# A gated graph network followed by graph attention: the product of softmax weights and rows of h in three passes

## The chip, the core and the metric

The kernel runs on one core of a Trainium2 chip. The metric is the device time of one execution in microseconds (us). One execution was also recorded by the hardware profiler; the profile and the trace below are of that execution.

A core has several engines that run side by side, each through its own instructions in a fixed order: PE (TensorE, the matrix unit), PEld (its weight loads, which overlap its products), ACT (ScalarE), DVE (VectorE), POOL (GpSimd), and SP (SyncE), which here issues DMA transfers. An engine waits at an instruction until the data it needs have been announced by the others; whatever stands behind that instruction on the same engine waits too. PSUM, the memory that PE writes, has eight banks here, each 128 x 512 floats.

## The reference

There are 64 graphs of 256 nodes with 256 features each, in float32. A first layer is a gated graph network of three steps, a second one is attention over the graph's edges; each has a normalization in front and adds its result to x. Cut to what matters:

```python
h = relu(layernorm(x))
for i in range(3):
    m    = h @ weight[i]
    aggr = einsum('bst,bsd->btd', A, m)          # A: adjacency, 0 or 1
    h    = gru_cell(aggr, h, w_ih, w_hh, b_ih, b_hh)
x = x + h

h  = relu(layernorm(x))
hW = einsum('bnd,od->bno', h, W)
e  = leaky_relu((hW @ a_left)[:, :, None] + (hW @ a_right)[:, None, :])
e  = where(adj == 0, -1e9, e)
alpha = softmax(e, axis=-1)
x = x + einsum('bij,bjd->bid', alpha, hW)
```

The kernel uses that alpha @ (h @ W.T) is (alpha @ h) @ W.T. The product of the softmax weights with the rows of h is called *mix* in the code, the following product with W *project*.

## The kernel before

The 64 graphs go through in 32 pairs (G = 2 graphs to a pair, N = 256 nodes, D = 256 features). A tile of 128 partitions by 512 elements holds one graph (two blocks of 128 nodes by 256 features) or half of the features of a pair.

Per pair, `pair(p)` records about these operations, none of which runs when it is recorded:

- `norm_relu` of the input and, for three layers, the state h split into parts (`split16`, names "h0", "h1"), the adjacency product ("prop", line 802, two per layer), its result split ("g0", "g1"), and the gates of the recurrent cell (`gate`, whose products are all line 665): per block of features r, nh, ni and z, with the arithmetic on ACT (lines 687, 820, 830, 833) and on DVE (lines 825, 828, 837 to 841).
- the attention part: `norm_relu` ("mid"), the dot products with the attention vectors (line 896), leaky relu, mask, maximum and exponentials of the scores, then a DMA transposition of the exponentials ("p turn") followed by two gathers and a copy on ACT that puts the two 16-bit halves of each number together ("p copy", the `join` of line 710). Its result is the tile `pT`: the turned, not yet normalized softmax weights.
- "mix" (line 953): for each of the two graphs, four float32 products of 128 x 128 weights (blocks of h, the tile `hb`) with 256 columns (of `pT`), summed in one PSUM bank, `pg`. The trace has two records for each float32 product of this kind.
- "c": `pg` split by `split16`: a part rounded to float32r on ACT (line 616), a float16 remainder on DVE (line 622), and a scaled float16 copy of the whole on ACT (line 627).
- "project" (line 964): the product with W in three passes, 4 products of float32r and 8 of float16, each of 256 columns. DVE multiplies the result with the reciprocal row sums, adds x (line 980), and the rows go out.

A *split in three passes* replaces a float32 product a*b by a0*b0 in float32r (a number rounded to fewer bits, in a 32-bit tile) plus two float16 passes for the remainders: a1 (the remainder of a) times a float16 copy of b, and the other way round. All gates, prop (with one float16 pass, since A is 0 or 1) and project work in this way before the change; mix doesn't. In a group with passes of both kinds (`mixed=True`), the order of the kinds alternates from group to group, so that PE switches type once in each group; the Python flag `narrow` keeps the state.

The last two pairs (p of 30 and 31, "late" and "last") use plain float32 for mix and for project (line 975), and the last pair has a code of its own (lines 1006 and 1014).

What sets the order: all operations go into a `Plan`, which is a list scheduler that runs when the kernel is built. It knows an assumed cost for each operation (the constants `MM`, `PROP`, `A512` and so on, in ns), the operations that each one needs, and the buffers ("full" 28, "round" 22, "half" 40, "bank" 8). It repeatedly takes the operation that can start first and, among equals, the one with the earliest due time; the table `LEAD` shifts the due time of operations by name. The result is a fixed sequence for each engine, and pairs overlap each other in it. So a changed cost or lead doesn't cost anything by itself: it moves instructions.

The core of the lines that the change replaces:

```python
            def mix(g=g, pT=pT, pg=pg):                                   # line 950
                for db in range(DB):
                    for jb in range(NB):
                        nc.tensor.matmul(...)                             # line 953
            pe(f"mix {g}", 4 * MM, mix, r=[(pT, ALL), (hb[g], ALL)], w=[(pg, ONE)])
            if p < NPAIR - 2:
                cs = split16(f"c{g}", pg, UP_V, True)
```

Of the kernel before, what the change touches and what calls it, by code (L numbers as in the profile page):

```python
# [10 lines left out]
F32 = mybir.dt.float32  # L11
# [19 lines left out]
    "A": -111500, "A16": -23000, "G": -500, "b_nh": -3500, "b_rz": 1000, "b_rz half": 7500, "back 0": 27500,  # L31
    "back 0 gather": 88000, "back 0 of 0": 32000, "back 0 of 1": 18000, "back 1": 28500, "back 1 gather": -33000,
    "back 1 of 0": -500, "back 1 of 1": 20500, "back copy 0": -80500, "back copy 1": -5000, "c0 0": -2500,
    "c0 1": 36500, "c0 d": 32000, "c1 1": 4000, "c1 d": 7000, "d add 0": -4000, "d add 0 of 0": -16000,
    "d add 1 of 0": -44000, "d add 1 of 1": -16000, "d mul 0": 125000, "d mul 0 of 0": -18500, "d mul 0 of 1": -5500,
    "d mul 1": 89000, "d mul 1 of 0": -24000, "d mul 1 of 1": -36000, "d sub 0": -17500, "d sub 0 of 0": -3000,
    "d sub 0 of 1": -19500, "d sub 1": -9000, "d sub 1 of 0": -38000, "d sub 1 of 1": 5500, "dot 0": -136000,
    "dot 1": 3500, "exps 0": 20000, "exps 0 0": 93000, "exps 1": 1000, "exps 1 0": -65000, "exps 1 1": -11500,
    "fill": 4000, "first A": 9000, "first A16": -17000, "first back 0": -34000, "first back 1": 16000,
    "first c0 0": -23000, "first c0 1": -26500, "first c0 d": 84500, "first c1 0": -83500, "first c1 1": -28500,  # L40
    "first c1 d": -2000, "first d add 0": 7000, "first d add 1": -4000, "first d mul 0": -84500,
    "first d mul 1": -6000, "first d sub 0": -44000, "first d sub 1": 1000, "first dot 1": 17500,
    "first exps 0": 8000, "first exps 1": -4000, "first fill": 35000, "first g0 0": -7000, "first g0 1": 69000,
    "first g0 d": -1000, "first g1 0": -8000, "first g1 1": 89500, "first g1 d": -21000, "first h0 0": 46000,
    "first h0 1": -4000, "first h0 d": 38000, "first h1 0": 44000, "first h1 1": -44500, "first h1 d": 32000,
    "first hi 0": -5500, "first hi 1": 10000, "first in 0 eps": -165000, "first in 0 pow": -11500,
    "first in 0 relu": 500, "first in 0 shift": 38000, "first in 0 stats": -16500, "first in 1 eps": -17000,
    "first in 1 pow": 2000, "first in 1 relu": 17000, "first in 1 shift": -21000, "first in 1 stats": 16000,
    "first in hi 0": -78500, "first in hi 1": 8000, "first in lo 1": 44500, "first leaky 0": 48000,
    "first leaky 1": -1500, "first line 0": -10000, "first line 1": 54000, "first lo 1": 76000, "first load": -18000,  # L50
    "first mask 0": 113000, "first mask 1": 32500, "first max 0": 16500, "first max 1": 9000,
    "first mid 0 eps": -31500, "first mid 0 pow": 3500, "first mid 0 relu": -5000, "first mid 0 shift": 500,
    "first mid 0 stats": 20500, "first mid 1 eps": -15000, "first mid 1 relu": 13000, "first mid 1 shift": -15000,
    "first mid 1 stats": 6000, "first mix 1": -29000, "first nh 0 scale": 32000, "first nh 1 scale": 8500,
    "first ni 0 topF": 28500, "first out 1": 4000, "first p copy 0": -72000, "first p copy 1": -25000,
    "first p turn 0 gather": -21000, "first p turn 1": -66000, "first p turn 1 gather": -1500,
    "first project 0": 32000, "first project 1": -3000, "first prop 0": 21000, "first prop 1": -12000,
    "first r 0 topF": -55500, "first r 0 topT": -47000, "first r 1": 31500, "first r 1 topF": 16000,
    "first r 1 topT": -52000, "first recip": 14500, "first res 0": 3500, "first right 0": 26000, "first store": -3500,
    "first tanh 0": -51500, "first tanh 1": -8000, "first total": -32000, "first turn 0": -153500,  # L60
    "first turn 1": 34500, "first turn copy 0": 33500, "first u 0": 12000, "first u 1": 16000, "first u add 0": -500,
    "first u add 1": -21500, "first z 0": -24000, "first z 0 topF": -32000, "first z 1": -33000,
    "first z 1 topF": -33500, "g0 0": 108000, "g0 1": 251500, "g0 d": 500, "g1 0": 6000, "g1 d": -49000,
    "h0 0": 39500, "h0 1": 50500, "h1 0": -43000, "h1 1": 311000, "h1 d": 112000, "hi 0": 3000, "hi 1": -7000,
    "in 0 eps": 39000, "in 0 pow": -1000, "in 0 relu": -124000, "in 0 stats": -49000, "in 1 eps": 7500,
    "in 1 pow": 17000, "in 1 relu": 19000, "in 1 shift": -14500, "in 1 stats": 323500, "in hi 0": -36000,
    "in hi 1": 40000, "in lo 0": -4000, "in lo 1": 33500, "last A": 18500, "last A16": 500, "last back 0": -94000,
    "last back 0 of 0": 1000, "last back 0 of 1": -1000, "last back 1": 24000, "last back 1 of 0": -55500,
    "last d add 0": 71500, "last d add 0 of 1": 27000, "last d add 1": 13000, "last d add 1 of 0": -2000,
    "last d add 1 of 1": 25000, "last d mul 0 of 0": 19000, "last d mul 0 of 1": -8000, "last d mul 1": -149500,  # L70
    "last d mul 1 of 0": -500, "last d mul 1 of 1": 6000, "last d sub 0": -34500, "last d sub 0 of 0": 7000,
    "last d sub 0 of 1": 37000, "last d sub 1": -20000, "last d sub 1 of 0": -74500, "last d sub 1 of 1": -111000,
    "last dot 0": -74000, "last dot 1": -7500, "last exps 0 0": 3000, "last exps 0 1": 1000, "last exps 1 0": -33500,
    "last exps 1 1": 120000, "last g0 0": -2500, "last g0 1": -30000, "last g0 d": -16000, "last g1 0": -50000,
    "last g1 1": 9000, "last g1 d": -39500, "last h0 0": -23500, "last h0 1": -33500, "last h0 d": -22000,
    "last h1 0": 41500, "last h1 1": 95500, "last h1 d": 31000, "last hi 0": 25500, "last hi 1": 16000,
    "last in 0 eps": -12000, "last in 0 pow": 34000, "last in 0 shift": 98000, "last in 0 stats": -52000,
    "last in 1 eps": -8000, "last in 1 pow": 87500, "last in 1 relu": 500, "last in 1 shift": -77500,
    "last in hi 0": -16500, "last in hi 1": 65000, "last in lo 0": -8000, "last in lo 1": 16000,
# [254 lines left out]
def tile_gated_gnn_then_gat(  # L334
# [106 lines left out]

    MM, TR, PROP, PASS = 432, 109, 120, 233
    PROP16, PASS16 = 110, 216
    A512, V512, S512, VP256, C512 = 475, 605, 660, 392, 522
    LINE, SPREAD, T16 = 4800, 4800, 1300
    SPLIT = 4096.0
    C = 1.0 / SPLIT
# [611 lines left out]
```

## Time and profile before

| What | Value |
|---|---|
| median of 3 runs (lowest to highest) | 1970.34 us (1968.96 to 1971.46) |
| the profiled execution's own time | 1970.78 us |
| its span, from first to last instruction | 1969.0 us |
| instructions in the span | 30480 |
| mean granted clock of TensorE | 0.997 |
| busy: DVE, ACT, POOL | 1548.4 us (79%), 1543.8 us (78%), 193.7 us (10%) |
| DMA, mean | 122 GB/s |

How to read it: the page gives each engine's busy time as a share of the span, then groups of like instructions (line of the code, engine, operation, tile written and tiles read, shape, count, total and mean time, idle time before them and what ended it), the waits, and the *chain*: the work that ended last, followed back from the last instruction to what released each step. Matmuls are pipelined, and a record's own duration covers its passage through the array; what a product takes of PE is the distance to the start of the next, and a piece of the chain gives that for a whole group. The trace can also be cut into windows of time with the busy time of each engine in each, and be listed in order of time.

### The profile page before, as it was taken

The page shows a single profiled execution, that of the slowest core. Times are in us where ns is not written, and L with a number is a line of the kernel's source. Part 1 is how long each engine was busy: PE and PEld are TensorE (multiplying, and loading weights), DVE is VectorE, ACT ScalarE, POOL GpSimd, SP SyncE. Part 2 cuts the span into 40 slices and gives each one's busy share as a digit, 9 for nine tenths or more (in the row PEclk, how much of TensorE's full clock was granted, in tenths as well). Part 3 has the DMA queues.
Part 4 walks back from the last instruction along what each step waited for, and adds up shares of the span by engine and source line. Part 5 has one row for each costly group of instructions (what it writes and reads, how often), then busy time and mean ns, then how long its engine had stood idle before and what let it go on. Part 6 is the DMA issues. An engine that isn't in the chain of part 4 may idle for free.

```text
span 1969.0 us, 30480 instructions
## 1 busy us (share of the span) xinstructions
PE 1953.8 (99%) x9965; PEld 1210.8 (61%) x9965; DVE 1548.4 (79%) x3714; ACT 1543.8 (78%) x2653; POOL 193.7 (10%) x262
## 2 busy tenths in 40 slices
PE   8999999999999999999999999999999999999998
PEld 5556665666665666656666656666656666566667
DVE  7687778778788777788787787787887787887776
ACT  5577887778887778887778887788777788777865
POOL 1001011011010011010010110110100110100000
PEclk9999999999999999999999999999999999999999
DMA  4256776667776687876687776677666768656632
GB/s 122 45 101 125 134 136 115 118 122 142 145 127 110 116 138 133 140 129 112 119 137 142 134 125 109 125 139 147 125 108 120 139 132 142 129 108 125 114 75 60
DMA packets 734463, 239.36 MB, mean 122 GB/s; under 512 B 658256, under 2 KB 734304, under 8 KB 734304
## 3 DMA queue, kind: packets, MB, share of 16 engines
q1 hardware_dynamic: 734272, 237.41, 65.8%
q8 instruction: 78, 1.28, 0.3%
q14 instruction: 81, 0.66, 0.2%
q10 hardware_dynamic: 32, 0.01, 0.0%
HBM read 61.09 MB, written 16.84 MB: 40 GB/s over the span
## 4 chain that ended last, share of the span: by engine, by line
PE 97%; DVE 2%; ACT 1%; issue 0%; DMA 0%; ACTq 0%; DVEq 0%
PE bank L665 77%; PE bank L802 9%; PE bank L953 6%; PE bank L964 4%; PE bank L592 0%; PE bank L868 0%; PE bank L519 0%; PE bank L975 0%; PE bank L1006 0%; PE bank L1014 0%; DVE full L839 0%; DVE full L544 0%; ACT full L738 0%; DMA rows<-in_L_gnn_b_hh_dram 0%; DVE full L841 0%
## 5 line engine op out<-in xcount | busy, mean ns | idle before, releaser
L665 PE MATMUL bank<-half,low_hh 128*128 128x512 f16 (+1 forms) x2328 | 613.9, 379 | 0.0
L665 PE MATMUL bank<-half,low 128*128 128x512 f16 (+1 forms) x2328 | 606.0, 378 | 0.0
L665 PE MATMUL bank<-round,fac_hh 128*128 128x512 f32 (+1 forms) x1164 | 398.7, 432 | 0.0
L665 PE MATMUL bank<-round,fac 128*128 128x512 f32 (+1 forms) x1164 | 393.5, 428 | 0.0
L710 ACT COPY full<-full 128x1024 uint16<-128x1024 uint16 x304 | 349.6, 1159 | 44.7 <-DMA full<-full 38.8
L665 PEld LDWEIGHTS <-low 128*128 128x128 f16 x2328 | 214.3, 98 | 273.9 <-issue 44.4
L665 PEld LDWEIGHTS <-low_hh 128*128 128x128 f16 x2328 | 198.4, 98 | 283.3 <-issue 101.5
L665 PEld LDWEIGHTS bank<-round,fac 128*128 128x128 f32 x1164 | 214.6, 189 | 58.1
L665 PEld LDWEIGHTS bank<-round,fac_hh 128*128 128x128 f32 x1164 | 214.5, 189 | 57.0
L732 POOL TENSOR_TENSOR small<-small,nhalf 128x2 f32<-128x2 f32 x128 | 103.8, 811 | 1456.8 <-DVE small L730 1398.3
L820 ACT ACTIVATE full<-bank,b_rz 128x512 f32<-128x512 f32 (+1 forms) x194 | 131.7, 680 | 104.7 <-PE bank L665 102.3
L833 ACT ACTIVATE full<-bank,b_rz 128x512 f32<-128x512 f32 (+1 forms) x194 | 131.8, 679 | 93.8 <-PE bank L665 93.4
L620 DVE TENSOR_TENSOR half<-bank,round 128x512 f16<-128x512 f32 x192 | 132.0, 688 | 75.2 <-ACT round L616 26.6
L825 DVE SCALAR_TENSOR_TENSOR full<-full,bank 128x512 f32<-128x512 f32 (+1 forms) x194 | 131.5, 678 | 61.2 <-ACT full L820 58.9
L830 ACT ACTIVATE full<-full,vec 128x512 f32<-128x512 f32 (+1 forms) x194 | 135.1, 710 | 56.1 <-DVE full L828 56.1
L616 ACT ACTIVATE round<-bank 128x512 fp32r<-128x512 f32 x252 | 150.9, 599 | 32.6 <-PE bank L802 31.5
L839 DVE SCALAR_TENSOR_TENSOR full<-full,full 128x512 f32<-128x512 f32 (+1 forms) x194 | 132.1, 681 | 55.1 <-ACT full L833 52.4
L652 DVE SCALAR_TENSOR_TENSOR half<-full,round 128x512 f16<-128x512 f32 x184 | 125.7, 684 | 57.5 <-ACT round L651 57.5
L627 ACT ACTIVATE half<-bank 128x512 f16<-128x512 f32 x252 | 144.5, 598 | 8.7 <-DVE half L620 6.3
L687 ACT ACTIVATE bank<-bank,b_nh 128x512 f32<-128x512 f32 (+1 forms) x194 | 125.6, 648 | 25.8 <-PE bank L665 25.5
L837 DVE TENSOR_TENSOR full<-full,full 128x512 f32<-128x512 f32 (+1 forms) x194 | 141.3, 739 | 4.3 <-ACT full L830 4.2
L828 DVE TENSOR_TENSOR full<-full,bank 128x512 f32<-128x512 f32 (+1 forms) x194 | 128.4, 673 | 17.5 <-PE bank L665 14.8
(106 smaller groups left out, 2465.9 us busy)
## 6 DMA issues: line engine op xcount, KB each, us to landing
full<-full SPq DMA_DIRECT2D x484, 128.0 KB, 3.5
x<-in_x_dram SPq DMA_DIRECT2D x64, 256.0 KB, 3.4
adj<-in_adj_dram SPq DMA_DIRECT2D x64, 256.0 KB, 3.4
full<-in_x_dram SPq DMA_DIRECT2D x64, 256.0 KB, 4.2
full<-full SPq DMA_DIRECT2D x248, 64.0 KB, 2.7
out_dram<-full SPq DMA_DIRECT2D x62, 256.0 KB, 2.9
full<-line SPq DMA_DIRECT2D x62, 128.0 KB, 4.3
full<-full SPq DMA_TRANSPOSE x304, 3.6
```

What stands on the lines that cost most here:

```text
L616: act(name + " 0", A512 if bank else C512, lambda: nc.scalar.activation(v0.t, v.t, AF.Copy, scale=up), r=[(v, ALL)], w=[(v0, ONE)])
L620: rem = lambda: nc.vector.tensor_sub(v1.t, v.t, v0.t.bitcast(F32))
L627: act(name + " d", A512, lambda: nc.scalar.activation(vd.t, v.t, AF.Copy, scale=up * C), r=[(v, ALL)], w=[(vd, ONE)])
L665: return [(j, lambda start, j=j, kb=kb: nc.tensor.matmul(bank.t[:, cols], fs(j, kb), s[kb][j].t[:, cols], start=start, stop=True, skip_gro ...
L710: act(name, 1065, lambda: nc.scalar.copy(dst.t.bitcast(U16).rearrange("p (j n b) -> p j n b", j=2, b=2), src.t.bitcast(U16).rearrange(f"p ...
L802: nc.tensor.matmul(pa.t[:, ts(g, N)], b, m[:, ts(sb, N)], start=(n == 0), stop=True, skip_group_check=True)
L820: act(f"r {db}{of}", fit(575, part), lambda b=r_, k=pr, db=db, cols=cols: nc.scalar.activation(b.t[:, cols], k.t[:, cols], AF.Tanh, bias=b ...
L825: dve(f"u {db}{of}", fit(S512, part), lambda u=u, k=ph, b=r_, cols=cols: nc.vector.scalar_tensor_tensor(u.t[:, cols], b.t[:, cols], 1.0, k ...
L830: act(f"tanh {db}{of}", fit(615, part), lambda u=u, en=en, cols=cols: nc.scalar.activation(u.t[:, cols], u.t[:, cols], AF.Tanh, bias=b_i[: ...
L833: act(f"z {db}{of}", fit(575, part), lambda b=z_, k=pz, db=db, cols=cols: nc.scalar.activation(b.t[:, cols], k.t[:, cols], AF.Tanh, bias=b ...
L837: dve2(f"d sub {db}{of}", fit(V512, part), lambda u=u, d=d, cols=cols: nc.vector.tensor_sub(d.t[:, cols], d.t[:, cols], u.t[:, cols]), r=[ ...
L839: dve2(f"d mul {db}{of}", fit(V512, part), lambda d=d, b=z_, cols=cols: nc.vector.scalar_tensor_tensor(d.t[:, cols], b.t[:, cols], 1.0, d. ...
```

## The change

For all pairs but the last two, mix is done in three passes. Two splits are added per graph, and the mix's result now carries a factor UP_H * UP_P = 2^25, which the scale of the following split "c" takes out again (the same instructions with another constant). A few assumed costs of the plan are changed, and the whole table of leads is a new one. The numbers of buffers are as before.

```diff
 LEAD = {
...
 }
...
-    A512, V512, S512, VP256, C512 = 475, 605, 660, 392, 522
+    A512, V512, S512, VP256, C512 = 477, 603, 603, 392, 521
...
+    UP_H, UP_P = 2.0**11, 2.0**14
...
-            act(name + " d", A512, lambda: nc.scalar.activation(vd.t, v.t, AF.Copy, scale=up * C), ...)
+            act(name + " d", A512, lambda: nc.scalar.activation(vd.t, v.t, AF.Copy, scale=up), ...)
...
-    def split16(name, v, up, bank=False, given=(None, None)):
+    def split16(name, v, up, bank=False, given=(None, None), part=None):
...
-        whole_of(name, v, vd, up, bank)
+        whole_of(name, v, vd, up * (part or C), bank)
...
-        dve(name + " stats", 1000, stats, ...)
+        dve(name + " stats", 880, stats, ...)
...
-                act(f"leaky {g}", 365, ...)
+                act(f"leaky {g}", 415, ...)
...
+            turned = lambda b: b.t.rearrange("p (i j n) -> p i j n", j=NB, n=P)
             if p < NPAIR - 2:
-                cs = split16(f"c{g}", pg, UP_V, True)
+                m0, m1, m2 = Buf("round"), Buf("half"), Buf("half")
+                act(f"m{g} 0", C512, ... nc.scalar.activation(b.t, v.t, AF.Copy, scale=UP_H), r=[(hb[g], ALL)], w=[(m0, ONE)])
+                dve2(f"m{g} 1", V512, ... nc.vector.scalar_tensor_tensor(
+                    b.t, v.t, UP_H, t.t.bitcast(F32), op0=ALU.mult, op1=ALU.subtract), r=[(hb[g], ALL), (m0, ONE)], w=[(m1, ONE)])
+                dve2(f"m{g} d", 340, ... nc.vector.tensor_copy(b.t, t.t.bitcast(F32)), r=[(m0, ONE)], w=[(m2, ONE)])
+                ps = split16(f"p{g}", pT, UP_P, part=1.0)
+
+                def mix(ms=(m0, m2, m1), ps=ps, pg=pg, turned=turned):
+                    js = (1, 2, 0) if narrow[0] else (0, 1, 2)
+                    for n, (j, db, jb) in enumerate((j, db, jb) for j in js for db in range(DB) for jb in range(NB)):
+                        nc.tensor.matmul(pg.t[:, ts(db, N)], parts(ms[j])[:, jb, ts(db, P)], turned(ps[j])[:, :, jb, :],
+                                         start=(n == 0), stop=True, skip_group_check=True)
+
+                pe(f"mix {g}", 4 * (PROP + 2 * PROP16), mix, mixed=True, r=[(b, ALL) for b in ps] + [(b, ONE) for b in (m0, m1, m2)], w=[(pg, ONE)])
+            else:
...
+                pe(f"mix {g}", 4 * MM, mix, r=[(pT, ALL), (hb[g], ALL)], w=[(pg, ONE)])
+            if p < NPAIR - 2:
+                cs = split16(f"c{g}", pg, UP_V / (UP_H * UP_P), True)
```

In the order that results mid-kernel, the two mixes of a pair stand back to back on PE, behind four groups of six gate products that follow the last of four props; the two projects follow after one group of twelve gate products.

## Prediction

> **What bounds the kernel now.** I read first the page's busy shares and its chain by line, then the waits of PE alone, then the chain's pieces and PE's list in order of time around one mix, last the windows.
>
> ```profile
> PE 1953.8 (99%) x9965; PEld 1210.8 (61%) x9965; DVE 1548.4 (79%) x3714; ACT 1543.8 (78%) x2653; POOL 193.7 (10%) x262
> ...
> PE 97%; DVE 2%; ACT 1%; issue 0%; DMA 0%; ACTq 0%; DVEq 0%
> PE bank L665 77%; PE bank L802 9%; PE bank L953 6%; PE bank L964 4%; PE bank L592 0%; PE bank L868 0%; PE bank L519 0%; PE bank L975 0%; PE bank L1006 0%; PE bank L1014 0%; DVE full L839 0%; DVE full L544 0%; ACT full L738 0%; DMA rows<-in_L_gnn_b_hh_dram 0%; DVE full L841 0%
> ```
>
> PE is both the busiest engine and 97% of the chain, so a product removed is time removed, if nothing new makes PE wait. PE's own waits:
>
> ```profile
> PE bank L495 <- DMA rows<-in_L_gnn_b_hh_dram: 4.9, 1, 4.9
> PE bank L868 <- DVE full L841: 3.6, 3, 1.8
> PE bank L853 <- DVE full L841: 2.3, 2, 1.8
> ```
>
> The columns are total us, times, longest. 4.9 us is the start; lines 868 and 853 are turns back of h for the first and the last pairs. Between these ends PE never waits. The chain (start, length, what) shows the period:
>
> ```profile
> 954.54 29.42 PE bank L665 x132
> ...
> 1014.33 29.42 PE bank L665 x132
> ```
>
> 1014.33 - 954.54 = 59.79 us per pair, without a gap. From the chain of the window around this pair's mix:
>
> ```profile
> 1003.65 3.46 PE bank L953 x16
> ...
> 1010.71 1.35 PE bank L964 x12
> ...
> 1012.99 1.34 PE bank L964 x12
> ```
>
> The two mixes take 3.46 us, 1.73 each. A project takes 1.345: it is 4 float32r and 8 float16 products of 128 x 256, exactly the form of the new mix.
>
> **The change, part by part.**
>
> *Mix on PE.* 30 pairs with 2 mixes each: 60 x (1.73 - 1.345) = 23.1 us less. Here a rule of the Trainium skill gives another figure. "FP8 and Floating Point Precision" (TensorE Precision Notes) says that true float32 is four passes through the array. Taken at its word, three passes cost three quarters: 1.73 / 4 = 0.43 saved per mix, 60 x 0.43 = 26 us. The trace has a pass in float32r dearer than one in float16: four of L802's float32r products stand 0.47 us apart from what follows (983.80 to 984.27), 0.117 each, against 1.73 / 16 = 0.108 for a float32 pass. 4 x 0.117 + 8 x 0.108 = 1.33, and a change of type makes it the 1.345 of the row. I take the row. A mixed group more per graph also means one switch from float32r to float16 more per pair. The stretch of 29.42 us holds 44 products of 0.2325 and 88 of 0.216, together 29.24; the rest, 0.18, is spread over some ten switches, 0.02 each. 30 x 0.02 = 0.6 back. PE's net: **-22.5 us**, 0.75 a pair, and a new period of 59.04.
>
> *Weight loads.* The float16 passes load their weights by instructions of their own, 16 more per pair. The same loads for project are 98 ns against a pitch of 108 ns and cost nothing there; uncovered they would cost 16 x 0.1 = 1.6 us a pair. Since project is the same form, I take zero.
>
> *Splits of h ("m") and of the weights ("p").* Per graph ACT gets two roundings (L616 from SBUF, 631 ns, pitch 0.52 in a row of two: 1.14 less 0.63), DVE two remainders (L622, 684 ns, pitch 0.60) and two float16 copies (L629, 416 ns, pitch 0.34). Per pair ACT +2.1 us, DVE 4 x 0.60 + 4 x 0.34 = +3.8. The windows say how much room there is (us, then busy of PE, PEld, DVE, ACT, POOL, then the granted clock, DMA share and rate):
>
> ```profile
> 277.40:337.20 59.80, 59.80 (x306) 36.71 (x304) 47.91 (x116) 48.33 (x84) 6.17 (x8) 1.00 0.71 129
> ...
> 1048.00:1058.00 10.00, 10.00 (x51) 5.82 (x50) 10.00 (x29) 9.03 (x17) 2.42 (x3) 1.00 1.27 197
> ```
>
> DVE goes from 47.9 of 59.8 to 51.7 of 59.0 (88%), ACT from 48.3 to 50.4 (85%). Both stay below PE, so they fit if they fall into the idle time; but the second line is a stretch of ten microseconds in which DVE is already full. The cover is PE's own queue of gates. Without it the cost is the whole path rounding, remainder, 0.63 + 0.68 = 1.3 us before each mix.
>
> *The new wait.* The first mix now waits on DVE (float16 parts of p) and ACT (its float32r part), where it waited for the join alone. Behind it on PE stand the second mix, twelve gate products and the two projects; for those wait the splits "c", the outputs, and the cell of another pair. In the changed order four groups of six gate products lie between the last prop and the first mix: 24 x 0.222 = 5.3 us of PE work. In it ACT rounds that prop's result (pitch 0.49), does the two joins (L710, 1159 ns, pitch 1.05) and the first rounding of p (0.63): 0.5 + 2.1 + 0.63 = 3.2, and DVE then the remainder: 3.9 us; the float16 copies need the join alone and go ahead. So the first mix has some **1.4 us to spare**; the second's operands come 0.6 later and its turn 1.35 later. The splits of h come right behind the second norm's relu, before dots, mask and softmax: no mix waits for them, and what they cost is room on DVE. I take zero for the wait, with bounds of nothing and a few tenths a pair.
>
> *Between mix and project.* After the first mix come 1.35 us of second mix and 12 x 0.222 = 2.7 of gates, 4.0 us, for ACT and DVE to split "c" (0.60 and 0.69). Before, 5.6 us lay there. Enough.
>
> *Buffers and queues.* Per pair 4 "round" and 8 "half" tiles more, out of unchanged pools; `hb` and `pT` in return needn't outlive their splits for the mix. PE waits for none of them now; I take zero, up to 0.3 a pair. The change issues no DMA, and SP's transfers keep their number; the leads move them relative to each other. ACT's joins waited for them at L710 for 38.8 us in 49 waits, at most 2.3.
>
> *Assumed costs and leads.* Stats, leaky and the rest change no instruction. They reorder the setup too: the turns of the weights come before most of the products of L592, and the sums of L609 later. PE is busy there from 5 to 47 us either way. What the seams cost is seen in the windows:
>
> ```profile
> 50.00:52.00 2.00, 1.30 (x6) 1.30 (x7) 2.00 (x5) 1.97 (x5) 0.00 (x0) 0.67 0.03 6
> 52.00:54.00 2.00, 2.00 (x10) 1.31 (x9) 1.38 (x3) 0.86 (x2) 0.00 (x0) 0.50 0.95 170
> ```
>
> Waits of 0.56 and 1.55 us at line 868 are followed by a clock of 0.67 and 0.50, which takes 2 x 0.33 + 2 x 0.5 = 1.7 us more. "TensorE: Matmul & The Clock Gate" (What's actually happening) lets the clock fall after an idle window of about 3.4 us; here 2.1 us in two pieces did it. By the rule a stall of this length costs itself, 2.1; by the trace 3.8, and I count stalls so. The new order has these turns at the same places (first pair, last drain), so I take no change, within 3 us either way.
>
> **Sum.** The profiled execution took 1970.78, its span 1969.0. Span 1969.0 - 22.5 = 1946.5, own time 1948.3. The median of the runs is 0.44 below the profiled one: **1947.9 us**.
>
> **Rivals.**
>
> A, the forecast: PE stays without gaps and gets its 22.5 us, ends within 3 us of now. 1945 to 1951. For it: no PE wait in 1,800 us, and an identical form in the trace. Chance 0.74.
>
> B, slower: the first mix waits for p. Place: PE before the first mix of each pair. The spare is 1.4 us and the gain 0.75, so B decides from a join 2.15 us later than the sum above; the longest DMA wait at L710 is 2.3. It also draws in the clock: a stall of 1.55 us, like that at line 868, with 1.7 of lost clock, less 0.75, is +2.5 a pair, 30 x 2.5 = +75: 2045 us. Against it: 49 waits in 304 joins, most of them short, and nothing in the order that makes each pair late. Chance 0.05.
>
> C, part of the gain is given back: DVE, full in stretches, hands a cell's result over late, and PE stands for 0.3 us in each pair. 30 x 0.3 = 9: 1957 us. For it DVE's 10.00 of 10 us; against it that DVE still waits at other times, and that the new leads spread the work. Chance 0.11.
>
> D, more than the sum: the new leads also close the waits at 868 and 853 (5.9 us, and 1.7 of clock after the first of them, of which half may go): 1944. Chance 0.08.
>
> E, the change doesn't bring its shorter mix: weight loads of the moving data's other layout (blocks of 128 with a stride) slow the passes to float32's 1.73. The old mix read the same blocks at full rate. 1970, chance 0.02.
>
> **How the numbers follow.** 1947.9 is A's. The range of 1943 to 1954 holds A, most of D and the nearer part of C; the rest of C, B and E is outside. About 0.2% (4 us) is what a measurement tells from no change. Faster by more: A, C, D = 0.93. Within: E = 0.02. Slower: B = 0.05.
>
> **What would show it.** Right: a period of about 59.0 us, the two mixes in a chain piece of 2.7, no new line in PE's waits, DVE near 88%. Wrong: PE waiting at mix for the remainder of p (B), at 665 for DVE (C), a granted clock below 1.00 mid-kernel, or mixes at 1.73 still (E).

## The result, and the profile after

| | before | after |
|---|---|---|
| median, same chip | 1969.65 us | 1958.0 us (1955.64 to 1959.96, 4 runs) |
| ratio, 95% interval | | 0.9927 [0.9912, 0.9942] |
| profiled execution, own time / span | 1970.78 / 1969.0 | 1956.43 / 1954.6 |
| PE busy | 1953.8 | 1930.9 |
| PE idle (span less busy) | 15.2 | 23.7 |
| DVE, ACT busy | 1548.4, 1543.8 | 1646.6, 1609.6 |

The change saves 11.7 us where 22.4 were forecast, and the time of 1958.0 lies outside the predicted range of 1943 to 1954. (The two profiled executions lie 14.4 us apart; the profiled one of the changed kernel is the second fastest of its four.) The table already tells where the rest is. PE's busy time fell by 22.9 us, close to the forecast's 22.5; PE's idle time rose by 8.5. So the products are about as cheap as predicted, and PE stands where it did not stand before.

Three lines of the page of the changed kernel (engine, busy time, share, instructions; then the chain of waits by engine and by line; the code has moved, so gates are now L668, props L805, mix L965, project L984):

```profile
PE 1930.9 (99%) x10205; PEld 1198.8 (61%) x10205; DVE 1646.6 (84%) x3954; ACT 1609.6 (82%) x2773; POOL 199.4 (10%) x262
...
PE 82%; ACT 6%; DMA 5%; DVE 5%; issue 1%; SPq 1%; ACTq 0%; DVEq 0%
PE bank L668 66%; PE bank L805 7%; DMA full<-full 4%; PE bank L965 3%; PE bank L984 3%; ACT full L713 2%; ACT round L619 1%; SPq L705 1%; PE bank L595 1%; DVE half L625 1%; ACT half L630 1%; DVE full L828 1%; ACT round L654 1%; DVE full L1000 1%; ACT full L741 0%
```

A "99%" for PE hides the loss; the chain shows it. Before, it ran through PE for 97%; now 18% of it runs through other engines, among them a transfer between two "full" tiles and L713, the copies that join the two 16-bit halves after a transposition (L710 before). The chain leaves PE only where PE had to wait. PE's waits (total us, times, longest):

```profile
PE bank L668 <- DVE half L625: 5.2, 10, 0.8
...
PE bank L1018 <- ACT full L1010: 3.2, 1, 3.2
PE bank L668 <- DVE half L623: 1.2, 2, 0.8
PE bank L805 <- DVE half L655: 0.4, 1, 0.4
```

Line 1018 is the last pair; the left-out rows are the start (L498) and the turns of h in the first and last pairs (L871). L668 for L625 is new: gates waiting for the remainder of h. There is no wait at L965, so the first mix never waits for the weights' split. The three mid-kernel rows sum to 6.8 us. The kernel before had one such row:

```profile
PE bank L802 <- DVE half L652: 0.2, 1, 0.2
```

Start and end took 0.5 and 1.1 us more; the last 0.3 of the 8.5 is in gaps too short for the list.

A pair without a stall is as forecast. From the chain of a window (start, length, what):

```profile
879.01 5.34 PE bank L668 x24
884.36 2.71 PE bank L965 x24
...
938.00 2.02 PE bank L668 x9
```

938.00 - 879.01 = 58.99 us (59.04 forecast), with the two mixes in 2.71 (2.7 forecast). Measured from project to project, half of the 25 regular periods (without those of the first and last pairs) are 58.98 to 59.15, and the others go up to 60.77. That longest one holds two stalls, 0.64 and 0.82 us, and is 1.78 longer: the stalls cost 1.46, and each costs 0.16 more. That is what the last product before a stall takes if it is paid in full (0.38 us as its record stands) and not at the pitch of 0.216; this part counts as busy. One period of 59.32 shows no idle time at all. Together the 25 periods are 10.7 us longer than 25 times 58.99.

What is late in the pair with the two stalls? The chain of a window around them, followed back from the gates at its end:

```profile
1004.50 5.40 DMA full<-full
...
1010.00 0.80 ACT full L713
...
1011.06 2.23 ACT full L713 x2
1013.29 1.05 ACT round L619 x2
1014.34 0.58 ACT full L823
...
1014.98 0.68 DVE full L828
...
1015.73 0.59 DVE half L625
1016.33 0.60 DVE full L842
1016.93 0.61 DVE half L625
...
1017.58 2.62 PE bank L668 x11
```

Read from the top: a gather lands 5.4 us after it was issued; ACT stands in a row of four joins ("back copy 0" of pair p, "turn copy 0" and "turn copy 1" of pair p+2, "back copy 1" of pair p) and waits there for the gather of the second. Behind the joins on ACT, without a hole, come the two roundings of h of pair p+2 and a tanh; behind that on DVE a gate's product, the first remainder of h (L625), another pair's product with z (L842) and the second remainder. The gate "nh 0" of pair p+2 on PE needs both. The pieces left out are at most 0.27 us each. From the gather's landing to the gate no engine in the row has anything else to wait for: whatever the gather is late by, beyond the spare, PE stands for.

Only three of the ten stalls for L625 have this chain. In the other seven the last steps ahead of L828 are on DVE. Around the stall at 483.34, a line of the trace in order of time and then pieces of the chain:

```profile
474.68 4.37 ACT L713 COPY full<-full 128x1024 uint16<-128x1024 uint16 x4 [2.04 <-DMA full<-full]
```

```profile
478.49 0.79 DVE full L1000 x2
479.28 0.67 DVE full L878 x2
479.94 0.66 DVE small L728 x2
...
480.74 0.68 DVE full L828
...
482.68 0.61 DVE half L625
```

The two ways run side by side. On ACT the roundings and the tanh follow the last join; on DVE it is followed by additions to x that need it (L878), behind outputs of graphs (L1000), and by a normalization (L728). Both are equally long to within 0.1 us: in all ten stalls L828 begins 1.7 us behind the end of the last join (479.05 here, 1013.29 above), and PE's gate 1.4 us (first remainder) or 2.6 us (second) behind that. **None of the instructions that the change adds is in either way.** Compare where the joins begin relative to the pair's first project. Pairs without a stall for L625 begin 1.3 to 0.2 us ahead of it, half of them 0.65 or more. Pairs with a stall begin 0.14 us ahead to 1.2 behind, but for one at 0.7 ahead, whose second join waits for its own gather. So the order has some 0.4 us to spare here.

Why is the gather late in the pair of the first chain? The same transfers in the same order take longer. Here is one window in that pair and one in a pair without a stall, each 2.7 us behind the issue of the first of six gathers (at 1002.31 and 884.28). The last three columns are granted clock, DMA share and GB/s:

```profile
1005.00:1007.00 2.00, 2.00 (x11) 1.16 (x9) 1.38 (x2) 1.17 (x3) 0.00 (x0) 1.00 1.44 128
```

```profile
887.00:889.00 2.00, 2.00 (x11) 1.14 (x10) 1.38 (x2) 1.56 (x4) 0.00 (x0) 1.00 0.87 128
```

At 128 GB/s in both, the packets took 1.44 times the window on the mean engine in one (they overlap) and 0.87 in the other. The 128 KB gathers around the first land after 4.8 us (median) against 3.3. The cause was not found.

### The profile page after: what moved, and what is told of

It is laid out like the page before. It is cut to its first block, busy times and chain, and to the rows that moved or that the text cites. A ratio compares the mean times of both kernels' runs of the same rounds, so it can differ in the third digit from the quotient of the medians.

```text
span 1954.6 us, 31416 instructions
## 1 busy us (share of the span) xinstructions
PE 1930.9 (99%) x10205; PEld 1198.8 (61%) x10205; DVE 1646.6 (84%) x3954; ACT 1609.6 (82%) x2773; POOL 199.4 (10%) x262
## 4 chain that ended last, share of the span: by engine, by line
PE 82%; ACT 6%; DMA 5%; DVE 5%; issue 1%; SPq 1%; ACTq 0%; DVEq 0%
PE bank L668 66%; PE bank L805 7%; DMA full<-full 4%; PE bank L965 3%; PE bank L984 3%; ACT full L713 2%; ACT round L619 1%; SPq L705 1%; PE bank L595 1%; DVE half L625 1%; ACT half L630 1%; DVE full L828 1%; ACT round L654 1%; DVE full L1000 1%; ACT full L741 0%
## 5 line engine op out<-in xcount | busy, mean ns | idle before, releaser
L668 PE MATMUL bank<-half,low_hh 128*128 128x512 f16 (+1 forms) x2328 | 621.7, 378 | 5.3 <-DVE half L625 5.2
L668 PE MATMUL bank<-half,low 128*128 128x512 f16 (+1 forms) x2328 | 620.5, 378 | 1.2 <-DVE half L623 1.2
L668 PE MATMUL bank<-round,fac_hh 128*128 128x512 f32 (+1 forms) x1164 | 433.4, 454 | 0.0
L668 PEld LDWEIGHTS <-low_hh 128*128 128x128 f16 x2328 | 211.1, 98 | 271.5 <-issue 64.9
L713 ACT COPY full<-full 128x1024 uint16<-128x1024 uint16 x304 | 342.5, 1162 | 37.1 <-DMA full<-full 23.4
L668 PEld LDWEIGHTS <-low 128*128 128x128 f16 x2328 | 203.3, 98 | 275.4 <-issue 83.2
L668 PE MATMUL bank<-round,fac 128*128 128x512 f32 (+1 forms) x1164 | 367.1, 405 | 0.0
L668 PEld LDWEIGHTS bank<-round,fac 128*128 128x128 f32 x1164 | 217.5, 188 | 56.4
L668 PEld LDWEIGHTS bank<-round,fac_hh 128*128 128x128 f32 x1164 | 212.8, 189 | 62.9
L735 POOL TENSOR_TENSOR small<-small,nhalf 128x2 f32<-128x2 f32 x128 | 122.2, 955 | 1243.3 <-DVE small L733 1239.1
L623 DVE TENSOR_TENSOR half<-bank,round 128x512 f16<-128x512 f32 x192 | 131.6, 687 | 59.8 <-ACT half L630 45.4
L625 DVE SCALAR_TENSOR_TENSOR half<-full,round 128x512 f16<-128x512 f32 x252 | 167.0, 682 | 2.4 <-ACT round L619 2.4
L655 DVE SCALAR_TENSOR_TENSOR half<-full,round 128x512 f16<-128x512 f32 x184 | 123.8, 688 | 46.4 <-ACT round L654 45.7
L630 ACT ACTIVATE half<-bank 128x512 f16<-128x512 f32 x252 | 146.4, 597 | 11.7 <-PE bank L805 11.2
L619 ACT ACTIVATE round<-bank 128x512 fp32r<-128x512 f32 x252 | 146.8, 597 | 10.2 <-PE bank L805 9.2
L840 DVE TENSOR_TENSOR full<-full,full 128x512 f32<-128x512 f32 (+1 forms) x194 | 132.3, 682 | 25.9 <-ACT full L833 25.9
L619 ACT ACTIVATE round<-full 128x512 fp32r<-128x512 f32 x252 | 146.2, 629 | 2.2 <-DVE full L844 2.0
L842 DVE SCALAR_TENSOR_TENSOR full<-full,full 128x512 f32<-128x512 f32 (+1 forms) x194 | 132.1, 681 | 11.7 <-ACT full L836 10.3
```

Of the source, the lines that this page charges most:

```text
L619: act(name + " 0", A512 if bank else C512, lambda: nc.scalar.activation(v0.t, v.t, AF.Copy, scale=up), r=[(v, ALL)], w=[(v0, ONE)])
L623: rem = lambda: nc.vector.tensor_sub(v1.t, v.t, v0.t.bitcast(F32))
L625: rem = lambda: nc.vector.scalar_tensor_tensor(v1.t, v.t, up, v0.t.bitcast(F32), op0=ALU.mult, op1=ALU.subtract)
L630: act(name + " d", A512, lambda: nc.scalar.activation(vd.t, v.t, AF.Copy, scale=up), r=[(v, ALL)], w=[(vd, ONE)])
L668: return [(j, lambda start, j=j, kb=kb: nc.tensor.matmul(bank.t[:, cols], fs(j, kb), s[kb][j].t[:, cols], start=start, stop=True, skip_gro ...
L713: act(name, 1065, lambda: nc.scalar.copy(dst.t.bitcast(U16).rearrange("p (j n b) -> p j n b", j=2, b=2), src.t.bitcast(U16).rearrange(f"p ...
```

## The experiments

Two theories were set against each other. LOAD is the predicted rival C: the added splits fill DVE (and ACT), so that a cell's result comes late. ORDER says that the added work is harmless, and that the new order, which the new leads and costs make, leaves no spare behind the joins, so that a late gather reaches PE. All ratios are to the kernel before on the same chip.

### Take the added work away, keep the order

The four added DVE operations of each graph do 64 of 512 columns (one of the four is shown):

```diff
-                dve2(f"m{g} 1", V512, ... nc.vector.scalar_tensor_tensor(b.t, v.t, UP_H, t.t.bitcast(F32), ...
+                dve2(f"m{g} 1", V512, ... nc.vector.scalar_tensor_tensor(b.t[:, :64], v.t[:, :64], UP_H, t.t[:, :64].bitcast(F32), ...
```

> Leaves out most of the four added DVE operations of each graph (64 of 512 columns are done; the order of all engines is that of the changed kernel). Theory LOAD (the added DVE work makes DVE late): PE's waits in mid-kernel, 6.8 us in the changed kernel's profile, fall under 1.5 us and the time falls by 5 to 8 us, to about 1951. Theory ORDER (the new order leaves no spare time behind four joins in a row, whatever the added work costs): PE's waits stay at 5 to 8 us and the time within 1955 to 1960.

Then the two roundings on ACT as well (one is shown; a scale of the split "c" is changed too, in the same instructions):

```diff
-                act(f"m{g} 0", C512, ... nc.scalar.activation(b.t, v.t, AF.Copy, scale=UP_H), ...
+                act(f"m{g} 0", C512, ... nc.scalar.activation(b.t[:, :64], v.t[:, :64], AF.Copy, scale=UP_H), ...
```

> As the run before, and the two added ACT roundings of each graph also do 64 of 512 columns, in the same order. LOAD: no PE wait left in mid-kernel, 1950 or a little less. ORDER: PE waits of 5 to 8 us stay, 1955 to 1960; a fall only here and not with DVE alone would say that ACT is the late one.

Measured: 1957.32 us, 0.9934 [0.9919, 0.9948], and 1957.14 us, 0.9928 [0.9913, 0.9943], against the changed kernel's 0.9927. DVE's busy time fell from 1646.6 to 1580.2 and then 1569.6, ACT's to 1571.1; PE still waits 7.1 and 5.4 us mid-kernel. Two thirds of the time that the change added on DVE are gone in the first, over three quarters in the second, with more than half of ACT's, and it brings nothing: LOAD is out.

### Each half of the change alone

The changed kernel with the table of leads from before:

```diff
 LEAD = {
-    "A": -93000, "A16": 28000, "G": -2000, ...
+    (the table of before)
```

> Mix in three passes as in the changed kernel, with the lead table of before. PE's busy time must be the changed kernel's (1931 us) under both. LOAD: PE waits of at least 6.8 us in mid-kernel again, since the work is the same, and 1956 or more. ORDER: the waits are a matter of the order and lie elsewhere; another sum, between 0 and 40 us, and 1950 to 1990.

The kernel before, with the new leads and assumed costs, and mix in float32 as it was:

```diff
-    A512, V512, S512, VP256, C512 = 475, 605, 660, 392, 522
+    A512, V512, S512, VP256, C512 = 477, 603, 603, 392, 521
 LEAD = {
+    (the table of after)
```

> Mix in float32 as before, with the new lead table and assumed costs. LOAD: PE has no waits in mid-kernel and the time is that of before, 1968 to 1972. ORDER: an order that these leads make for other work has waits behind joins in mid-kernel, 3 us or more in all, and 1972 or more.

The first took 1966.87 us, 0.9981 [0.9973, 0.9989] (20 runs, 1962 to 1973): with the old leads about three quarters of the gain are lost. It was a partial miss, since PE's busy time was 1937.3 and not 1931. Its trace has 5.0 us of mid-kernel waits, fewer than the changed kernel's 6.8, so what it loses lies elsewhere; that was not followed. The second took 2000.22 us, 1.0156 [1.0139, 1.0173]. PE's largest mid-kernel waits in it (mix is L955 there, the joins L712):

```profile
PE bank L955 <- ACT full L712: 7.0, 9, 1.2
PE bank L804 <- DVE half L654: 4.5, 5, 1.2
```

A kernel without a single added instruction, but in another order, has some 16 us of mid-kernel waits, the largest row of them for a join. So waits of this size need only an order. (It is 29 us slower than the kernel before, more than these waits; PE's busy time is 7.6 us higher too.) Neither run proves which order is at fault in the changed kernel, as each order is a new one.

### Lengthen the row, shorten the row

If the row from the joins to the gates (by either way) has no spare, its length must go straight into the time. To lengthen it, the last "back copy 1" of each pair copies half its columns twice, some 0.55 us of ACT, with nothing else moved:

```diff
-    def join(name, src, dst, order="b j n"):
+    def join(name, src, dst, order="b j n", twice=False):
...
+            for part in [slice(None)] + [slice(0, 1)] * twice:
+                nc.scalar.copy(...[:, part], ...[:, part])
...
-                    join(f"back copy {db}", rs, hn)
+                    join(f"back copy {db}", rs, hn, twice=last and db == 1)
```

> The changed kernel in its own order, with the last of the four joins in a row (the turn back of the second half of h, last layer) copying half of its columns a second time: about 0.55 us more on ACT per pair, the result is the same. Theory ORDER-NO-SPARE (in the new order the joins, the rounding of h and its remainder stand in one row ahead of a gate, with some 0.4 us to spare in an undisturbed pair): PE's mid-kernel waits go from 6.8 to 12 to 17 us, at the same line, in about 20 pairs in place of 10, and the time rises by 5 to 10 us to about 1965. Rival (the transfers themselves, or DVE, are what is late, and ACT's join isn't on that path): ACT has idle time right before the joins, so no change, 1955 to 1960.

Measured 1969.67 us, 0.9998 [0.9988, 1.0009]. The row of PE's waits that was 5.2 us and 10 times is now:

```profile
PE bank L668 <- DVE half L625: 15.2, 26, 1.4
```

Seventeen microseconds more on ACT (busy 1627.0 against 1609.6), an engine with 18% idle time, undo the whole change: 26 stalls in place of 10, the longest 1.4 us against 0.8. The waits are in the expected range; the time rose by more than was expected, 11.7 us and not 5 to 10.

To shorten it, the two roundings (L619) and remainders (L625) of h behind the joins do 64 of 512 columns:

```diff
-            hs = [split16(f"h{db}", hT[db], UP_V, given=given[db]) for db in range(DB)]
+            hs = [split16(f"h{db}", hT[db], UP_V, given=given[db], k=64 if i == 0 and p > 2 else GN) for db in range(DB)]
```

> The changed kernel in its own order, but for pairs 3 to 31 the two splits of h in the pair's first step (the roundings right behind the four joins, and the remainders behind them) do 64 of 512 columns; their other columns are not computed. It is the counterpart of the longer join: the row from the joins to PE's first gate becomes some 0.85 us shorter on ACT and up to 0.9 on DVE, and the longest stall there is 0.83. ORDER WITHOUT SPARE: the waits of L668 for L625 go from 6.4 us to under 1, mid-kernel waits from 6.8 to under 2, time 1951 to 1954. If something else sets the stalls (the outputs on DVE, or the joins alone beyond the spare), they stay above 4 us and the time at 1957 to 1959.

Measured 1952.27 us, 0.9903 [0.9889, 0.9916]:

```profile
PE bank L668 <- DVE half L625: 1.4, 4, 0.4
```

The time is as expected. The waits are 3.0 us mid-kernel where under 2 were: L625 keeps 1.4, those for L623 and L655, of another row, stay (0.8 and 0.6), and 0.3 is at the mix. Compare this with taking the *added* work away: there eight operations a pair on DVE and four on ACT were thinned and nothing moved; here it is two on each (which of them counted is seen in the next run). It is the place that counts.

One shortening missed. The outputs (L1000), which stand in DVE's way to L828, were cut to 32 of 256 columns:

```diff
-                    parts(b)[:, nb, :], pv.t[:, ts(nb, D)], sm.t[:, 8 + nb : 9 + nb], parts(b)[:, nb, :],
+                    parts(b)[:, nb, :32], pv.t[:, nb * D : nb * D + 32], sm.t[:, 8 + nb : 9 + nb], parts(b)[:, nb, :32],
```

> Leaves out most of the last operation of each graph (x plus the product with W times the reciprocal row sums: 32 of 256 columns are done); the order is that of the changed kernel. Four such DVE operations stand between the joins and the remainder of h. ORDER-NO-SPARE: where the row goes by DVE (the first three waits of the changed kernel's profile) it gets 1 us shorter, where it goes by ACT not; PE's mid-kernel waits go from 6.8 to 3 to 5 us, 1954 to 1957. Rival (the transfers alone): 6 to 8 us, no change.

1958.75 us, 0.9938 [0.9923, 0.9954], with 8.8 us of mid-kernel waits: no gain. The expectation had read rightly that the first chains go by DVE. But behind the outputs DVE needs the last join, and ACT's way beside it is as long: L828 now begins 1.66 us behind the last join, in place of 1.70. The short roundings show the same from the other side. There L828 still begins 1.69 us behind the last join, by DVE's way, and what became shorter is the piece from L828 to PE, 1.67 us in place of 2.60. So the remainders, which both ways share, gave the gain at these places, and the roundings on ACT nothing.

### Move a join to GpSimd

POOL is busy 10% of the time, so one join of the row, then two, were given to it:

```diff
-    def join(name, src, dst, order="b j n"):
+    def join(name, src, dst, order="b j n", aside=False):
+        eng = nc.gpsimd.tensor_copy if aside else nc.scalar.copy
...
-                    join(f"back copy {db}", rs, hn)
+                    join(f"back copy {db}", rs, hn, aside=last and db == 1)      # then: aside=last
```

> The changed kernel in its own order, but the last of the four joins in a row (turn back of the second half of h, last layer) is copied by POOL, which is busy 10% of the time, and not by ACT; the result is the same. ORDER-NO-SPARE with the row going by ACT (joins, two roundings of h, a tanh, then DVE's remainder): the row gets 1.06 us shorter, so that only the pairs with the latest transfers still hold PE up; mid-kernel waits of PE from 6.8 to between 1 and 3 us, 1951 to 1954. Rival (DVE's own queue or the transfers set the time, ACT's row only stands beside them; or POOL's copy comes later than ACT's): waits of 6 us or more, 1957 or more.

> As the run before with both joins of the last layer's turn back on POOL, one after the other. ORDER-NO-SPARE: ACT's row is 2.1 us shorter, but the first of these joins stands first in DVE's queue (the addition to x), so this gains over the run before only if POOL's copy takes about as long as ACT's; 1950 to 1956. Rival: as above, 1957 or more, and more with POOL slower than ACT.

Both missed widely: 1994.76 us, 1.0118 [1.0103, 1.0133], and 1987.93 us, 1.007 [1.0045, 1.0096]; PE waits for L625 30.1 us in 38 stalls with one join moved. A stretch of the trace in order of time shows what happened:

```profile
486.32 1.15 POOL L713 COPY full<-full 128x1024 uint16<-128x1024 uint16 x1 [23.69 <-DMA full<-full]
...
486.59 2.09 DVE L632 TENSOR_SCALAR half<-full 128x512 f16<-128x512 f32 x1
...
487.41 0.99 POOL L893 MEMSET full<- 128x512 f32 x2
```

POOL's copy takes 1.15 us, as ACT's did. But the float16 copy on DVE that begins in it (L632, 0.43 us when alone, as at 485.46 in the same stretch) ends only at 488.68, once POOL's copy and the fills behind it are over. Not every DVE instruction is held up: two outputs (L1000) run into the same copy of POOL's at 486.32 and take 0.87 us together, as they do in the changed kernel. Over the kernel the mean of L632 rises from 463 to 559 ns. Everything behind it on DVE, the remainders of h among it, is late by that. So the row became shorter on ACT and longer on DVE (33 of the 38 chains go by DVE); these two runs say nothing for or against ORDER.

### Other orders

Three kernels with the changed kernel's instructions, in other orders. The first has a table of leads searched for an order that, by the plan's own costs, also holds when gathers land later:

```diff
 LEAD = {
-    "A": -93000, "A16": 28000, "G": -2000, ...
+    "A": -108500, "A16": -18500, "G": -9000, ...
```

> The changed kernel with another table of leads, searched for an order that also holds when the gathers land 0.4 to 1.4 us later than planned. In the resulting order the gates' products that need the new h come behind the ones that don't (ni ahead of nh), and one join stands between the two roundings. All instructions are those of the changed kernel. ORDER WITHOUT SPARE: mid-kernel waits 0.5 to 3 us, time 1949 to 1954, below the changed kernel's 1958. If late transfers are not what makes the waits, or another order meets as many new ones: mid-kernel waits 6 or more, time 1957 or above.

The second swaps two groups of six products on PE, once per pair:

```diff
             # PE, per pair
-            z 1 (pair p+1), nh 0 (p+2), ni 0 (p+2), r 0 (p+2)
+            z 1 (pair p+1), ni 0 (p+2), nh 0 (p+2), r 0 (p+2)
```

> The changed kernel with one swap on PE per pair (29 in all): where the six products of nh 0, which need the new h, stand right ahead of the six of ni 0, which need the adjacency result that has been there for 15 us, ni 0 goes first. Every other instruction of every engine keeps its place. The row of joins, roundings and remainders gets 1.33 us of spare that way, the longest stall there is 0.83. ORDER WITHOUT SPARE: the waits of L668 for L625 and for L623 vanish (under 0.5 us), mid-kernel waits 0.2 to 1.5, time 1950 to 1953: the predicted gain but for the ends. What it costs: ACT's scale of nh 0 and all behind it come up to 1 us later, without a wait of PE in the plan. If the stalls only move to another place (mid-kernel waits above 4), the time stays at 1956 to 1959.

The third leaves PE alone and swaps five pairs of neighbours on ACT and DVE:

```diff
+SWAPS = [
+    ("ACT", ("back copy 1", 1), ("exps 1", 1), -2), ("ACT", ("back copy 1", 1), ("in hi 1", 1), 1),
+    ("DVE", ("d mul 0", 2), ("h1 1", 1), 1), ("DVE", ("mask 1", 1), ("max 0", 1), 0), ("DVE", ("max 1", 1), ("in 1 shift", 1), 3),
+]
```

(engine, operation and its occurrence in the pair, its right neighbour and occurrence, how many pairs the neighbour is ahead).

> The changed kernel with five swaps of neighbours per pair, on ACT and DVE alone; PE, SP and POOL keep their order and every instruction is there. On ACT the second back copy of h's first step, which waits for a gather at the head of a row of some ten microseconds without a hole, goes behind the exponential and the rounding of the next input (in hi 1) that stand behind it. On DVE the second remainder of h (h1 1, L625) goes ahead of d mul 0 (L842), and two reductions of the softmax swap with their neighbours. ORDER WITHOUT SPARE: both places where PE stood (L668 for L625; L668 for L623 with L805 for L655) get a spare of 0.6 to 2 us: mid-kernel waits from 6.8 to under 2 us, PE's busy time stays at 1931, time 1949 to 1953, ratio to before about 0.990. If the stalls move on to a third place, as with ni first, mid-kernel waits stay above 4 and the ratio at 0.993 or above.

*Searched leads*: 1962.05 us, 0.9953 [0.994, 0.9967]. The waits went as expected, to 2.0 us mid-kernel, and the time did not: PE's busy time is 1941.6, 10.7 more for the same products. The chain shows where:

```profile
947.70 1.60 PE bank L965 x12
...
950.62 1.37 PE bank L965 x12
951.99 1.52 PE bank L984 x12
...
954.86 1.35 PE bank L984 x12
```

This order puts a group of gates between the two mixes and between the two projects. The four groups together take 1.60 + 1.37 + 1.52 + 1.35 = 5.84 us, where the changed kernel has 2.71 + 2.70 = 5.41 for them back to back. The period is 59.44 against 58.99.

*ni first*: 1959.78 us, 0.994 [0.9928, 0.9953], a miss of the time. The waits for L625 are gone, as expected, but:

```profile
PE bank L668 <- DVE half L623: 5.1, 7, 0.8
...
PE bank L805 <- DVE half L655: 3.0, 7, 0.6
```

The second and third kind of stall of the changed kernel grew, and mid-kernel waits are 8.1 us in all. The chain of this kernel ahead of one of them:

```profile
1160.02 5.15 DMA full<-full
...
1165.19 1.18 ACT full L713
1166.37 1.00 ACT full L936 x4
...
1175.91 0.70 DVE half L623
1176.65 1.50 PE bank L668 x6
```

It is a second row of the same build: a gather that landed after 5.15 us, a join ("back copy 1" of the first step), then ten microseconds of ACT instructions without a hole down to the split that PE waits for. Moving nh 0 on PE does nothing for this row; why it stalls more often here than in the changed kernel (7 times against 2) was not followed further.

*Five swaps*: **1947.39 us** (1944.7 to 1949.92), 0.9888 [0.987, 0.9905]; the interval lies below the changed kernel's. They give both places a spare: the late join at the head of ACT's ten microseconds goes behind two ready operations, and the second remainder of h, which ends the first row, goes ahead of L842. A line of its page, and the only row of PE's waits between the ends:

```profile
PE 1927.0 (99%) x10205; PEld 1198.0 (62%) x10205; DVE 1659.2 (85%) x3954; ACT 1614.7 (83%) x2773; POOL 211.6 (11%) x262
```

```profile
PE bank L668 <- DVE half L625: 0.4, 2, 0.2
```

0.4 us of mid-kernel waits are left of 6.8. The instructions are the changed kernel's, DVE and ACT are busy no less than there, PE, SP and POOL keep their order, the pools of buffers are the same, and the lost time is back. Could the transfers simply have become faster with the swaps? The 128 KB gathers land after 3.6 us (median) in both kernels, and a join still waits up to 3.0 us:

```profile
ACT full L713 <- DMA full<-full: 13.9, 19, 3.0
```

That settles it for ORDER. The expectation was still too cautious: the time is below its 1949 to 1953, and PE's busy time fell to 1927.0 where it was to stay at 1931. Over the same thirty projects the kernel is 9.2 us shorter than the changed kernel (1713.9 against 1723.1): 6.5 of idle time, and 2.7 that the records count as busy, of which the products paid in full before a stall are a part.

## Why the prediction was wrong

**PE's own sum was right.** Mix 60 x 0.385 less 0.6 for the switches gave -22.5; the two mixes of a pair went from 3.46 to 2.71 us, 30 x 0.75 = 22.5, and the period is 58.99 for 59.04. The row priced it and not the rule of four equal passes, which would have given 26. Weight loads at zero were right: the mix takes 1.355. That PE's busy time shows -22.9 is in part luck: the stalls add to it what the products before them take in full, and one dip of the granted clock less takes 1.7 away. The five swaps, with hardly a stall and two dips less, show 1927.0, or -26.8; without the dips that is -23.4.

**The splits were sized about right and do fit.** DVE rose by 98.2 us, 3.3 a pair (3.8 forecast), ACT by 65.8, 2.2 a pair (2.1). Thinning them gains nothing, so they cost PE nothing.

**The new wait at the first mix, and the way from mix to project, were right**: no wait at L965 or L984 in the changed kernel. Rival B's place never mattered.

**The step that failed is "Buffers and queues"**, with its "the leads move them relative to each other" followed by "I take zero, up to 0.3 a pair", and with it forecast A's "PE stays without gaps". The 38.8 us in which joins waited for transfers were quoted there and taken as harmless, as PE had no gap at the time. In the old order they did reach PE nowhere but for 0.2 us. In the changed kernel joins wait for transfers *less*:

```profile
ACT full L713 <- DMA full<-full: 23.4, 30, 2.0
```

Yet these waits cost more, because joins now stand at the head of rows without a hole. The term was 30 x 0. Measured, PE's waits at L668 and L805 are 6.6 us longer than before, 0.22 a pair, and with the part that counts as busy the 25 regular periods lose 10.7 us, 0.43 each. That is more than the bound of 0.3, and the range did not even take in the bound. The buffers, the other half of that paragraph, are not to blame: the five swaps get the time back out of the same pools.

**Rival C had the size and the wrong cause.** 1957 us from 0.3 us a pair at the gates, and "PE waiting at 665 for DVE" as its sign, is what came (1958.0). But DVE's fullness from the added splits, its reason, is refuted by the thinned kernels. (In seven of the ten stalls DVE has no hole ahead of the gate, but with work that it had before.) DVE hands the result over late since it gets it late from ACT's joins, and ACT from a gather. A wait of PE put down to DVE named only the last link.

**Seams**: no change within 3 us was right. The start takes 0.5 more and the end 1.1. Before, the granted clock falls to 0.50 for 3.4 us three times (at 50.7, 1924.6 and 1948.5 us), in the changed kernel's trace twice (at 1909.9 and 1940.6; a third dip begins 0.3 us before the end), which is 1.7 us less. The prediction counted a stall of 2.1 us at 3.8, clock included. That is no fixed price: waits of 0.21 and 1.87 us at the place of the first dip bring none in the changed kernel, and 0.22 and 1.86 bring one in the kernel with short roundings.

What stays open: why the same gathers take 5 us in some pairs and 3.3 in others. Some pairs are hit again and again: stalls near 246, 1017, 1433 and 1534 us stand in the traces of the changed kernel, of both thinned ones and of the one with narrow outputs. The five swaps make PE nearly indifferent to it; they don't explain it.

## What to carry to other kernels

When PE (or any bound engine) has no gap, ask of each hand-over how much spare it has, not only whether it waits now: a change that rearranges a list schedule can leave every price right and take the spare from behind a transfer whose time varies. Follow a new wait back to the first link that varies, in several of the stalls and not in one: where two ways of equal length run side by side, shortening one gives nothing, and only what they share counts. Test by lengthening and shortening the row: half a microsecond of ACT a pair there was worth the whole gain, while 115 us of work taken off DVE and ACT elsewhere were worth nothing. An order searched on assumed costs should be replayed with late transfers before it is trusted, and with the real price of what it puts next to what on the bound engine.

## What the runs showed of the hardware

- **A copy on POOL holds up some DVE instructions.** L632 took 2.09 us in place of 0.43 while POOL copied and filled, but two L1000 that ran into the same copy took their usual 0.87. The Trainium skill ("Trainium Architecture — The Big Picture", What this means for kernel authors) calls the port pair that the two share an exclusive lock and no split of bandwidth; the trace agrees for L632, as this copy on DVE ended only when POOL was done.
- **The same products cost PE more between other neighbours**: four groups of twelve, 5.84 us with gates in between against 5.41 back to back.
- **A stall costs more than its idle time**: 1.78 us longer for 1.46 idle, the clock staying at 1.00. With the longer join, 1.26 and 0.83 us of idle time at 1445 to 1448 us were followed by 3.4 us at a clock of 0.50.
- **Equal gathers differ**: 4.8 against 3.3 us to land, at a DMA share of 1.44 against 0.87 with 128 GB/s moved in both.
